# Row maxima of an attention kernel: one transpose of 32 columns in place of four of 8

## The chip, the core and the metric

The kernel runs on one core of a Trainium2 chip. A core has TensorE (PE, matrix products into PSUM; PEld is its loading of the stationary operand), VectorE (DVE), ScalarE (ACT), GpSimd (POOL) and SyncE (SP); transfers between memories are issued from SP, ACT and POOL into queues. Each engine works off its own instructions in order and waits on semaphores for the others. The metric is the device time of one execution in microseconds (us); a lower one is better.

## What is computed

A transformer block on x of shape (2, 1024, 512): layer normalisation, causal attention with 32 heads of 16 and ALiBi biases, and a gate from an octonion feed-forward network with ternary weights. Cut to what matters:

```python
xn = _layernorm(x, axis=-1)
qkv = jnp.einsum('bsd,od->bso', xn, w_qkv) + b_qkv
scores = jnp.einsum('bhqd,bhkd->bhqk', q, k) * scale      # scale = 1/4
scores = scores + alibi[None, :, None, :]                 # per head and key position
scores = jnp.where(causal, scores, -1e9)
attn = jax.nn.softmax(scores, axis=-1)
out = jnp.einsum('bhqk,bkhd->bqhd', attn, v)
s = out @ w_out.T + b_out
g = silu(octonion_ffn(xn))          # gate, up and down with ternary weights
x = x + s * g
```

The case concerns the maximum that the softmax subtracts from each row of scores, and how it gets to where the second score product can use it.

## The kernel before

**Tiling.** Attention is cut into 32 units (b, g, qc): 2 batches, 8 groups of 4 heads, 2 halves of 512 query rows. The scores of a unit are computed twice. The first time (`max_items`, matmul at L537) queries are on the partitions: a tile of 128 queries against up to 512 keys for one head or more. VectorE adds the causal mask on the diagonal block and reduces each row to its maximum. `left` handles the keys of the first half (for qc = 1), `diagonal` the half that has the diagonal. Both write one column for each tile `tl` (4 tiles of 128 queries) and head `i` (4 heads) into small tiles `left` and `mx` of 128 x 16.

The second time (`exp_step`, matmul at L653) keys are on the partitions and queries in the free dimension, so that the result can go straight into the product with the values (`value_step`, L689) after the exponential on ScalarE. The row maximum is subtracted inside this product: the query stack `q_ring` is a tile of 128 rows x 4 heads x 512 queries, whose last two rows (126 and 127, `NR - 2` and `NR - 1`) hold the maxima as a rounded high part and a remainder, against rows of -1 in the key stack. The first product uses rows 0 to 125 only, the second all 128.

**The path of the maxima.** `split_max` joins `mx` and `left` and writes high part and remainder into `rm` on VectorE. `place_max` turns `rm` on TensorE (queries come to lie along the free dimension), copies the result from PSUM to `mr` in SBUF on ScalarE, and issues two transfers on POOL that put the high parts into row 126 of the query stack and the remainders into row 127. The first `exp_step` of the unit waits for both.

**The order.** Instructions of all engines in the attention stage are emitted in one program order that a planner in the kernel computes as it builds the program. It keeps a book of modelled times: `now` for PE, `act`, `dve`, when PSUM buffers come free (`e_free`, `x_free`, `m_free`), and for every unit `placed`, when its maxima lie in the query stack. In each step it takes, among the first products (`next_max`), the second products (`next_exp`), the value products (`next_value`), the turns (`next_turn`: placing maxima, normalising outputs), the projections (`next_side`) and the weight work (`next_behind`), one that is ready soon, by priority. Fills of the query and key stacks on SP (`fill_q`, `fill_k`), the loads of the next projection weights on ACT's queue and the stores of projections follow from the position that the planner has reached. The book entries for `place_max` are in `next_turn`: 436 ns on PE, 150 ns later 500 ns on ACT, and 3500 ns more until the maxima are placed.

**Behind the attention stage** the gated network runs (L1387 gate and up, L1421 down), from about 850 us to the end, without the planner.

Every ACT, DVE, POOL and SP instruction of the first two thirds is issued by a wrapper, so the profile gives all of them one line, L69; they are told apart by their tiles. Matmuls have their own lines. The transposes of `place_max` stand at L602 (`pm` is the PSUM tile, `mr` the copy, `q_stack<-mr` the transfer).

Of the kernel before, what the change touches and what calls it, by code (L numbers as in the profile page):

```python
# [10 lines left out]
F32 = mybir.dt.float32  # L11
F32R = mybir.dt.float32r
BF16 = mybir.dt.bfloat16
AF = mybir.ActivationFunctionType
ALU = mybir.AluOpType
AX = mybir.AxisListType
# [3 lines left out]
P = 128  # L20
# [55 lines left out]
def kernel(  # L76
# [18 lines left out]
    nc = tc.nc  # L95

    held = [True]
    act_, dve_, pool_, sp_ = (
        InOrder(tc, engine, held) for engine in (nc.scalar, nc.vector, nc.gpsimd, nc.sync)
    )  # L100
# [3 lines left out]
    def pe(ins):  # L104

        return tc.keep_in_program_order(ins)
# [14 lines left out]
    wk = ctx.enter_context(tc.tile_pool(name="wk", bufs=2))  # L121
# [5 lines left out]
    ident = const.tile([P, P], F32, name="ident")  # L127
# [86 lines left out]
    for n in range(2):  # L214
        for i in range(4):
            sp_.dma_start(
                out=bqk_sb[n * 64 + i * HD : n * 64 + (i + 1) * HD, :, :],
                in_=bqk[i * 32 : i * 32 + HD, :].rearrange(
                    "d (w g n) -> d w g n", w=2, n=2
                )[:, :, :, n],  # L220
# [177 lines left out]
    def q_of(b, g, half):  # L398
        return q_ring[(2 * (b * NG + g) + half) % 4]

    def k_of(b, g, half):
        return k_ring[(2 * (b * NG + g) + half) % 5]
# [122 lines left out]
    def max_items(b, g, qc):  # L525

        tiles = {}

        def begin():
            for name in ("left", "mx")[1 - qc :]:  # L530
                tiles[name] = wk.tile([P, 4, 4], F32, tag=name, name=f"{name}_{b}_{g}_{qc}")

        def products(tl, first, count, c, n):
            ps = ps_x.tile([P, 512], F32, tag="x", name=f"s1_{b}_{g}_{4 * qc + tl}_{c}_{first}")
            for j in range(count):
                pe(
                    nc.tensor.matmul(  # L537
                        ps[:, j * n : (j + 1) * n],
                        lhsT=q_of(b, g, qc)[0 : NR - 2, first + j, tl * P : (tl + 1) * P],
                        rhs=k_of(b, g, c)[0 : NR - 2, first + j, :n],  # L540
                        start=True,
                        stop=True,
                    )
                )
            return ps[:, 0 : count * n].rearrange("p (h n) -> p h n", n=n)

        def left(tl, i):
            if (tl, i) == (0, 0):
                begin()
            ps = products(tl, i, 1, 0, 512)  # L550
            dve_.tensor_reduce(tiles["left"][:, tl, i : i + 1], ps, AX.X, ALU.max)

        def diagonal(tl, first, count):
            if (qc, tl, first) == (0, 0, 0):
                begin()
            n = (tl + 1) * P
            ps = products(tl, first, count, qc, n)
            block = ps[:, :, tl * P : n]
            dve_.tensor_tensor(
                block,  # L560
                block,
                mask[:, 384:512].rearrange("p (h n) -> p h n", h=1).to_broadcast([P, count, P]),
                ALU.add,
            )
            dve_.tensor_reduce(
                tiles["mx"][:, tl, first : first + count], ps, AX.X, ALU.max
            )

        items = []
        for tl in range(4):  # L570
            if qc:
                for i in range(4):
                    items.append((1, 512, False, lambda tl=tl, i=i: left(tl, i)))
            count = (4, 2, 1, 1)[tl]
            for i in range(0, 4, count):
                items.append(
                    (
                        count,
                        (tl + 1) * P,
                        True,  # L580
                        lambda tl=tl, i=i, count=count: diagonal(tl, i, count),
                    )
                )
        return items, tiles

    def split_max(b, g, qc, tiles):

        mx = tiles["mx"]
        if qc:
            dve_.tensor_tensor(mx, mx, tiles["left"], ALU.max)  # L590
        rm = wk.tile([P, 4, 2, 4], F32, tag="rm", name=f"rm_{b}_{g}_{qc}")
        tiles["rm"] = rm
        dve_.tensor_copy(rm[:, :, 0, :].bitcast(F32R), mx)
        dve_.tensor_tensor(rm[:, :, 1, :], mx, rm[:, :, 0, :], ALU.subtract)

    def place_max(b, g, qc, tiles):

        q = q_of(b, g, qc)
        ps = ps_m.tile([P, 512], F32, tag="m", name=f"pm_{b}_{g}_{qc}")
        for tl in range(4):  # L600
            pe(
                nc.tensor.transpose(  # L602
                    ps[0:8, tl * P : (tl + 1) * P],
                    tiles["rm"][:, tl].rearrange("p l h -> p (l h)"),
                    ident,
                )
            )
        mr = wk.tile([8, 512], F32R, tag="mr", name=f"mr_{b}_{g}_{qc}", bufs=1)
        act_.copy(mr, ps[0:8, :])
        for n in range(2):  # L610
            pool_.dma_start(
                out=q[NR - 2 + n : NR - 1 + n].bitcast(F32),
                in_=mr[4 * n : 4 * n + 4, :].bitcast(F32),
            )

    p_tiles, po_tiles = {}, {}
# [85 lines left out]
    def normalise(b, g, qc):  # L702

        posb = po_tiles.pop((b, g, qc))
        o = op.tile([P, 4, 64], F32, tag="o", name=f"o_{b}_{g}_{qc}")
        pt = ps_m.tile([P, 4, 4, 32], F32, tag="m", name=f"pt_{b}_{g}_{qc}")
        for tl in range(4):
            pe(
                nc.tensor.transpose(
                    pt[:, tl, :, :].rearrange("p h e -> p (h e)"),  # L710
                    posb[:, tl * P : (tl + 1) * P],
                    ident,
                )
            )
        rl = wk.tile([P, 4, 4, 1], F32, tag="rl", name=f"rl_{b}_{g}_{qc}")
        dve_.reciprocal(rl, pt[:, :, :, HD : HD + 1])
        dve_.tensor_tensor(
            o.rearrange("p t (h d) -> p t h d", d=HD),
            pt[:, :, :, 0:HD],
            rl.to_broadcast([P, 4, 4, HD]),  # L720
            ALU.mult,
        )
        n = b * (S // P) + 4 * qc
        sp_.dma_start(
            out=att[n : n + 4, :, g * 64 : (g + 1) * 64].rearrange("t p n -> p t n"), in_=o
        )
# [78 lines left out]
    for u in range(NU):  # L805
        its, t = max_items(*units[u])
# [27 lines left out]
    for b in range(B):  # L834
        for hh in range(2):
            n = 2 * b + hh
# [11 lines left out]
        for gp in range(2 - 2 * b, NP):  # L848
            n = b * NP + gp
# [7 lines left out]
        for n, qc in enumerate((0, 1) if b + 1 < B else (1, 0)):  # L857
            u = (b + 1) * 2 * NG + n

            first, last = (u - 1, u) if b + 1 == B else (u + 8 + 4 * n, u + 12 + 4 * n)  # L860
# [191 lines left out]
    now, kind = [0.0], ["F"]  # L1052
    act, dve = [0.0], [0.0]
    e_free, x_free, m_free = [0.0] * 3, [0.0] * 2, [0.0] * 2
# [6 lines left out]
    def take(pool):  # L1061
        pool.sort()
        return pool

    def run_pe(k, ready, cost):
        now[0] = max(ready, now[0] + SWITCH.get((kind[0], k), 0)) + cost
        kind[0] = k

    def run_act(t, cost):
        act[0] = max(act[0], t) + cost  # L1070
        return act[0]

    def run_dve(t, cost):
        dve[0] = max(dve[0], t) + cost
        return dve[0]
# [79 lines left out]
    def next_turn():  # L1155
        found = []
        if turns:
            u, t = turns[0]

            def go(u=u):  # L1160
                turns.pop(0)
                place_max(*units[u], mtiles[u])
                run_pe("F", ready, 436)
                take(m_free)[0] = run_act(now[0] + 150, 500)
                placed[u] = m_free[0] + 3500

            ready = max(t, min(m_free))
            found.append((ready, 1, 0, go))
        if norms:
            u, t = norms[0]  # L1170

            def go(u=u):
                norms.pop(0)
                normalise(*units[u])
                run_pe("F", t2, 436)
                take(m_free)[0] = run_dve(now[0] + 150, 600)
                stored[units[u]] = m_free[0] + 5000

            t2 = max(t, min(m_free))
            found.append((t2, 2, 0, go))  # L1180
        return [f for f in found if f[0] < HELD]
# [132 lines left out]
    left = [RUN]  # L1314
# [13 lines left out]
    for t in [  # L1328
# [9 lines left out]
        t = t.rearrange("p h n -> p (h n)")[:, 0 : 12 * P]  # L1338
# [122 lines left out]
    for n, (tb, mt) in enumerate(work):  # L1461
# [11 lines left out]
        if n >= 2:  # L1473
            while last_outs:
                _, emit, kind = last_outs.pop(0)
# [76 lines left out]
```

## Time and profile before

| what | us |
|---|---|
| median of 3 runs | 1151.21 (1150.77 to 1151.92) |
| the profiled execution | 1150.65 |
| its span from the first to the last instruction | 1148.9 |
| PE busy | 1067.9 (93%) |
| DVE busy | 679.0 (59%) |
| ACT busy | 500.9 (44%) |
| POOL busy | 176.8 (15%) |
| ACT copies mr<-pm, 32 of 572 ns | 18.3 |
| PE transposes pm<-ident,rm, 128 of 281 ns, overlapping | 20.1 |
| POOL issues q_stack<-mr, 64 of 505 ns | 32.0 |

The mean granted TensorE clock is 0.978. Busy shares are averages over the whole span; PE's is above 0.8 in nearly all 40 slices of the page, that of the others changes with the stage. Durations of matmuls overlap each other, since they are pipelined; what one costs in a row of others is read from the starts in the timeline. `x <- y` in a row is an instruction or transfer that writes tile x and reads y, followed by its shape; `[t <-w]` behind a row is the idle time of the engine before it and what ended it. A chain is followed back from the last instruction, at each step to what released it.

### The profile page before, as it was taken

What the parts mean: (1) busy time and instruction counts of PE and PEld (TensorE: products, weight loads), DVE (VectorE), ACT (ScalarE), POOL (GpSimd) and SP (SyncE); (2) the same over time, 40 slices, a digit from 0 to 9 for tenths busy, and PEclk for the clock granted to TensorE, in tenths of its full rate; (3) what the DMA queues carried; (4) which work ended last, traced back from release to release, by engine and by line L of the source; (5) the groups of instructions that cost most, each with busy time, mean ns of one, the idle gap of its engine ahead of it and who ended that gap; (6) DMA issues with size and microseconds to landing.
All of it is one profiled execution on the core that took longest, in us unless ns stands there. A gap on an engine that the chain in (4) does not pass through costs nothing.

```text
span 1148.9 us, 15597 instructions
## 1 busy us (share of the span) xinstructions
PE 1067.9 (93%) x5562; PEld 680.9 (59%) x5562; DVE 679.0 (59%) x1400; ACT 500.9 (44%) x962; POOL 176.8 (15%) x295
## 2 busy tenths in 40 slices
PE   7979979999999999989999999899889999999996
PEld 5644545664555665545565555555446687878784
DVE  5368787667777687767787768777641123141211
ACT  4122656645554544535435444465582122232222
POOL 6401023100011010010110000001001123242322
PEclk9899979999999999989999999999899999999998
DMA  6975563453744608082542542831041013030200
GB/s 194 206 147 142 112 169 85 69 87 90 140 112 88 127 2 158 2 195 38 140 66 52 102 90 85 142 62 52 25 140 68 29 45 110 1 110 1 76 35 37
DMA packets 73740, 104.24 MB, mean 91 GB/s; under 512 B 26992, under 2 KB 31120, under 8 KB 73664
## 3 DMA queue, kind: packets, MB, share of 16 engines
q1 hardware_dynamic: 66336, 87.48, 34.8%
q10 hardware_dynamic: 3552, 9.78, 2.7%
q0 software_dynamic: 3776, 5.98, 2.1%
q8 instruction: 45, 0.74, 0.3%
q14 instruction: 31, 0.25, 0.1%
HBM read 69.58 MB, written 33.10 MB: 89 GB/s over the span
## 4 chain that ended last, share of the span: by engine, by line
PE 67%; DVE 12%; DMA 9%; ACT 5%; issue 5%; POOL 2%; SPq 1%; ACTq 0%; DVEq 0%; POOLq 0%
PE s L537 11%; PE s L653 11%; PE po L689 11%; PE pqk L466 6%; PE pg L1387 6%; PE pu L1387 6%; PE pd L1421 5%; DVE mx L69 5%; PE pout L758 4%; DMA q_stack<-mr 3%; PE pv L424 3%; DVE s L69 2%; PE s L670 2%; DVE left L69 1%; ACT p L69 1%
## 5 line engine op out<-in xcount | busy, mean ns | idle before, releaser
L69 ACT ACTIVATE p<-s 128x512 f32<-128x512 f32 x576 | 302.3, 599 | 222.7 <-PE s L670 142.0
L537 PE MATMUL s<-k_stack,q_stack 126*128 126x512 f32 (+3 forms) x768 | 276.3, 417 | 28.2 <-DVE mx L69 22.4
L653 PE MATMUL s<-q_stack,k_stack 128*128 128x512 f32 (+3 forms) x768 | 221.5, 373 | 17.3 <-DMA q_stack<-mr 12.9
L69 DVE TENSOR_REDUCE mx<-s 128x1 f32<-128x384 f32 (+3 forms) x352 | 226.2, 643 | 11.7
L69 DVE TENSOR_REDUCE left<-s 128x1 f32<-128x512 f32 x256 | 169.0, 686 | 86.2 <-PE s L537 85.2
L537 PEld LDWEIGHTS s<-k_stack,q_stack 126*128 126x128 f32 x768 | 133.1, 193 | 128.6 <-issue 33.3
L653 PEld LDWEIGHTS s<-q_stack,k_stack 128*128 128x128 f32 x768 | 135.2, 192 | 74.4 <-ACT p L69 30.2
L69 DVE TENSOR_TENSOR s<-s,mask 128x128 f32<-128x128 f32 (+2 forms) x352 | 124.2, 353 | 62.2 <-PE s L537 61.1
L689 PE MATMUL po<-p,v 128*32 128x512 f32 (+3 forms) x1536 | 143.0, 491 | 0.1
L466 PE MATMUL pqk<-xnT,wq 128*128 128x512 f32 x256 | 131.3, 614 | 4.5 <-POOL wq L69 2.2
L69 DVE SCALAR_TENSOR_TENSOR h<-pu,sc_u,sg 128x512 f32<-128x512 f32 (+1 forms) x44 | 33.1, 751 | 166.1 <-PE pu L1387 158.7
L69 POOL DMA_DIRECT2D q_stack<-mr x64 | 32.0, 505 | 583.6 <-ACT mr L69 583.6
L689 PEld LDWEIGHTS po<-p,v 128*32 128x32 f32 x1536 | 43.4, 109 | 78.8 <-issue 67.3
L69 POOL TENSOR_TENSOR hs<-h,hs 128x512 fp32r<-128x512 f32 (+1 forms) x44 | 57.6, 1309 | 190.1 <-ACT hs L69 190.1
L69 ACT ACTIVATE sg<-pg,sc_g 128x512 f32<-128x512 f32 (+1 forms) x44 | 30.2, 687 | 100.2 <-PE pg L1387 95.3
L424 PE MATMUL pv<-wv,xnT 128*128 128x256 f32 x256 | 68.2, 383 | 1.5 <-DVE v L69 1.5
L758 PE MATMUL pout<-wo_sb,oT 128*128 128x512 f32 x128 | 61.1, 597 | 2.0 <-ACT oT L69 1.0
L466 PEld LDWEIGHTS pqk<-xnT,wq 128*128 128x128 f32 x256 | 47.1, 198 | 26.6 <-issue 18.1
L69 ACT CAST hs<-h 128x512 fp32r<-128x512 f32 (+1 forms) x44 | 27.3, 620 | 75.3 <-DVE h L69 75.3
L670 PE MATMUL s<-mask,ident 128*128 128x256 bf16 (+1 forms) x320 | 52.0, 257 | 0.0
L424 PEld LDWEIGHTS pv<-wv,xnT 128*128 128x128 f32 x256 | 45.8, 190 | 9.8 <-issue 3.2
L69 ACT CAST mr<-pm 8x512 fp32r<-8x512 f32 x32 | 18.3, 572 | 70.7 <-PE pm L602 67.2
(142 smaller groups left out, 1081.1 us busy)
## 6 DMA issues: line engine op xcount, KB each, us to landing
sp<-st SPq DMA_DIRECT2D x32, 512.0 KB
k_stack<-sp SPq DMA_DIRECT2D x128, 128.0 KB
q_stack<-sp SPq DMA_DIRECT2D x128, 128.0 KB
wqr<-in_wqk_dram ACTq DMA_DIRECT2D x16, 512.0 KB
xt<-in_x_dram SPq DMA_DIRECT2D x16, 256.0 KB
att<-o SPq DMA_DIRECT2D x32, 128.0 KB
ot<-att SPq DMA_DIRECT2D x16, 256.0 KB
proj<-y SPq DMA_DIRECT2D x16, 256.0 KB
```

The source lines that it names most:

```text
L69: ins = issue(*args, **kwargs)
L424: nc.tensor.matmul(ps[:, 0:256], lhsT=xnT[:, c, b * S + kt * P : b * S + (kt + 1) * P], rhs=wv_tiles[2 * b + hh][:, c, :], start=(c == 0), ...
L466: nc.tensor.matmul(ps, lhsT=wq_tiles[b, gp][:, kt, which, :], rhs=xnT[:, kt, b * S + c * 512 : b * S + (c + 1) * 512], start=(kt == 0), st ...
L537: nc.tensor.matmul(ps[:, j * n : (j + 1) * n], lhsT=q_of(b, g, qc)[0 : NR - 2, first + j, tl * P : (tl + 1) * P], rhs=k_of(b, g, c)[0 : NR ...
L653: nc.tensor.matmul(ps[:, c0 : c0 + w], lhsT=k_of(b, g, kt // 4)[0:NR, h, kt % 4 * P : (kt % 4 + 1) * P], rhs=q[0:NR, h, 512 - w : 512], st ...
L670: pe(nc.tensor.matmul(out, lhsT=ident16, rhs=rhs, start=False, stop=True))
L689: nc.tensor.matmul(po[32 * i : 32 * i + 32, 512 - w : 512], lhsT=v[:, kt, h * VC : h * VC + 32], rhs=p[:, i * part + c0 : i * part + c0 + ...
L758: nc.tensor.matmul(ps, lhsT=turned[t][:, c, :], rhs=wo_sb[0][:, c, :], start=(c == 0), stop=(c == KD - 1),)
L1387: nc.tensor.matmul(ps[:fs, :], lhsT=fw[mt][:, n0 + kt, 0:fs], rhs=part[:, kt, :], start=(kt == 0 and n == 0), stop=(kt == KD - 1 and n == 1),)
L1421: nc.tensor.matmul(pd, lhsT=hs[k][:fs, n, st * P : (st + 1) * P], rhs=fw[mt][:fs, 8:12, :].rearrange("p s n -> p (s n)"), start=(mt == 0 a ...
```

## The change

The 16 columns of maxima are laid out head first, tile last, in place of tile first. `rm` becomes 2 parts x 4 heads x 4 tiles, contiguous: 32 columns that one transpose turns into 32 rows of 128. Before, four transposes turned 8 columns each (2 parts x 4 heads of one tile) into 8 rows x 128 at four places of the free dimension. The copy to SBUF is 32 x 128 in place of 8 x 512. The two transfers each read 16 rows of 128 numbers in place of 4 rows of 512; where they write is the same. The planner's entries for the turn become 109 ns on PE and 200 ns on ACT. No engine's other instructions are edited; their order is what the planner makes of the new entries.

```diff
@@ left, diagonal @@
-            dve_.tensor_reduce(tiles["left"][:, tl, i : i + 1], ps, AX.X, ALU.max)
+            dve_.tensor_reduce(tiles["left"][:, i, tl : tl + 1], ps, AX.X, ALU.max)
...
-                tiles["mx"][:, tl, first : first + count], ps, AX.X, ALU.max
+                tiles["mx"][:, first : first + count, tl], ps, AX.X, ALU.max
@@ split_max @@
-        rm = wk.tile([P, 4, 2, 4], F32, tag="rm", name=f"rm_{b}_{g}_{qc}")
+        rm = wk.tile([P, 2, 4, 4], F32, tag="rm", name=f"rm_{b}_{g}_{qc}")
         tiles["rm"] = rm
-        dve_.tensor_copy(rm[:, :, 0, :].bitcast(F32R), mx)
-        dve_.tensor_tensor(rm[:, :, 1, :], mx, rm[:, :, 0, :], ALU.subtract)
+        dve_.tensor_copy(rm[:, 0].bitcast(F32R), mx)
+        dve_.tensor_tensor(rm[:, 1], mx, rm[:, 0], ALU.subtract)
@@ place_max @@
-        for tl in range(4):
-            pe(
-                nc.tensor.transpose(
-                    ps[0:8, tl * P : (tl + 1) * P],
-                    tiles["rm"][:, tl].rearrange("p l h -> p (l h)"),
-                    ident,
-                )
-            )
-        mr = wk.tile([8, 512], F32R, tag="mr", name=f"mr_{b}_{g}_{qc}", bufs=1)
-        act_.copy(mr, ps[0:8, :])
+
+        pe(nc.tensor.transpose(ps[0:32, 0:P], tiles["rm"].rearrange("p l h t -> p (l h t)"), ident))
+        mr = wk.tile([32, P], F32R, tag="mr", name=f"mr_{b}_{g}_{qc}", bufs=1)
+        act_.copy(mr, ps[0:32, 0:P])
         for n in range(2):
             pool_.dma_start(
                 out=q[NR - 2 + n : NR - 1 + n].bitcast(F32),
-                in_=mr[4 * n : 4 * n + 4, :].bitcast(F32),
+                in_=mr[16 * n : 16 * n + 16, :].bitcast(F32),
             )
@@ next_turn @@
                 place_max(*units[u], mtiles[u])
-                run_pe("F", ready, 436)
-                take(m_free)[0] = run_act(now[0] + 150, 500)
+                run_pe("F", ready, 109)
+                take(m_free)[0] = run_act(now[0] + 150, 200)
                 placed[u] = m_free[0] + 3500
```

## The prediction

> **What bounds the kernel now.** I read the page's chain of waits first, to see which engine sets the end, then the group rows of the turned tile, then the chain piece by piece in stretches of 100 us, last the timeline around single placements.
>
> ```profile
> PE 67%; DVE 12%; DMA 9%; ACT 5%; issue 5%; POOL 2%; SPq 1%; ACTq 0%; DVEq 0%; POOLq 0%
> PE s L537 11%; PE s L653 11%; PE po L689 11%; PE pqk L466 6%; PE pg L1387 6%; PE pu L1387 6%; PE pd L1421 5%; DVE mx L69 5%; PE pout L758 4%; DMA q_stack<-mr 3%; PE pv L424 3%; DVE s L69 2%; PE s L670 2%; DVE left L69 1%; ACT p L69 1%
> ```
>
> TensorE holds two thirds of the chain, and one transfer, the placement of the row maxima (q_stack<-mr), stands in it with 3%. The attention stage runs from about 50 to 850 us. The table of windows over it gives 747 us of busy PE in 800, so 53 us of idle at most. A matmul instruction taken away there should mostly shorten the kernel; what shortens only ACT or POOL should not.
>
> ```profile
> L602 PE MATMUL pm<-ident,rm x128: 269/272/421, 69.9 to 826.5; 128*8 128x128 f32 x128
> L69 ACT CAST mr<-pm x32: 558/575/579, 70.7 to 826.9; 8x512 fp32r<-8x512 f32 x32
> ```
>
> This view of the turned tile (min, median and max ns; first and last start in us) shows 128 transposes and 32 copies. A transpose lasts 272 ns, but they overlap, so the timeline must say what four cost:
>
> ```profile
> 498.16 0.60 PE L602 MATMUL pm<-ident,rm 128*8 128x128 f32 x4
> ...
> 498.59 1.02 PE L466 MATMUL pqk<-xnT,wq 128*128 128x512 f32 x2
> ...
> 499.66 0.98 POOL L69 DMA_DIRECT2D q_stack<-mr  x2 [6.36 <-ACT mr L69]
> ...
> 507.11 1.19 PE L653 MATMUL s<-q_stack,k_stack 128*128 128x512 f32 x2 [3.56 <-DMA q_stack<-mr]
> ```
>
> Four transposes hold PE from 498.16 until the next matmul starts at 498.59, 0.43 us. The copy starts when the last has ended, POOL issues two transfers, and at 507.11 PE has stood still for 3.56 us until they landed.
>
> ```profile
> 498.24 0.53 PE pm L602 x4
> ...
> 498.79 0.58 ACT mr L69
> ...
> 500.15 6.83 DMA q_stack<-mr
> ```
>
> These are the chain's pieces at the same placement (start, length): transposes, copy and transfer are all on it. The same view, asked for the whole stage in stretches, has the transposes on the chain at 24 of the 32 units (1 unit is one placement), the copy at 10 and the transfer at 7.
>
> **The change part by part.** *TensorE.* Three of four transposes of each unit go, 96 in all. At the eight placements for which I asked the timeline, four take 0.35 to 0.44 us to the next matmul's start, so one takes 0.09 to 0.11 and three fewer give 0.26 to 0.33; I take 0.30. The one that stays loads 32 columns in place of 8: nearest rows 86 ns for 8 and 110 ns for the 32 columns of the value products (po); 24 ns more, under the running matmul. 24 units on the chain x 0.30 = 7.2 us. The other 8, where the chain runs through VectorE, give 0 to 0.33 each; I take 0, since another engine ends last.
>
> *ScalarE.* The copy goes from 8x512 to 32x128. Its nearest row is the 80x128 cast out of PSUM of the down weights (md), 263 ns: 572 - 263 = 0.31 us less, 32 times. ACT has idle time enough, so only the chain counts. At three of its ten places there (160.15, 173.77 and 826.85) the next link is again work of PE or ACT: 3 x 0.31 = 0.9 us.
>
> *The seven placements that PE waits for.* Transposes and copy together bring the issue 0.30 + 0.31 = 0.61 us forward.
>
> ```profile
> q_stack<-mr POOLq DMA_DIRECT2D x64, 8.0 KB, 1.8
> ...
> mw<-md POOLq DMA_DIRECT2D x4, 40.0 KB, 1.9
> ```
>
> The usual landing is 1.8 us, but the seven on the chain take 3.69 to 6.83 us: they share the DMA engines with bulk traffic (the DMA share is 1.1 in 500 to 510 us). If the landing follows the issue, each gives 0.61; if it comes when the bulk has drained, 0, and the 0.30 counted above for the six of them with transposes on the chain is lost again. I take the middle: 7 x 0.31 / 2 = 1.1 us gained, 6 x 0.30 / 2 = 0.9 us taken back.
>
> *The transfers.* Two per unit as before, on POOL, from 16 rows of 512 B in place of 4 rows of 2 KB. The second row above, of 80 rows of 512 B bounds it: it lands 0.1 us later, and its issue takes 0.56 us beside 0.50. So 0 to 0.1 us in landing and 0 to 0.12 in the two issues, at seven places 0 to 1.5 us; 16 rows are nearer to 4 than to 80, I take 0.2. Queued behind them on POOL are only weight repacking and memsets, with 583.6 us of idle in front of these transfers. Queue 0 shows 64 packets for the two transfers of one placement (549 to 555 us), 32 each. A rule speaks against the change here: the Trainium skill, "DMA: Bandwidth & Descriptors", section "Why a DMA increments its semaphore by 16 and not by 1", spreads data over as many engines, up to 16, as divide the slowest dimension on both sides, which could make 4 rows use 4 engines and 16 rows up to 16, to wait for the most backlogged of them. The same section lets all 16 engines report the end of a transfer issued from GpSimd whatever its shape, and 32 packets for 4 rows look like that; by the first alone the seven landings could lose what they gain, by the second nothing, and the sum stays.
>
> *VectorE.* The reductions write their columns with a stride, the split writes contiguously. The cast into the strided rm takes 175 ns, the contiguous maximum of mx and left 175 ns: nothing.
>
> *The planner.* Its book entries for one placement fall by 327 ns on PE and 300 on ACT, so every later greedy choice may fall differently, in all queues, SP's fills included. The trace of before cannot show the new order. Bounds from the waits:
>
> ```profile
> PE s L537 <- DVE mx L69: 22.4, 55, 3.3
> ...
> PE s L653 <- DMA q_stack<-mr: 12.9, 7, 3.6
> ```
>
> If the seven waits vanished, 12.9 us would go; if there were twice as many, 12.9 would come. I take 0 and keep both for the rivals.
>
> **Sum:** 7.2 + 0.9 + 1.1 - 0.9 - 0.2 = 8.1 us. The profiled execution took 1150.65 us (span 1148.9 and 1.75 around it); 1142.55 after. The median of the runs is 0.56 above it: 1143.1. Without the order, the ends are 18 x 0.26 - 1.5 = 3.2 us and 24 x 0.33 + 10 x 0.31 + 8 x 0.33 = 13.7 us: 1137.5 to 1148.
>
> **The rivals.** *A, slower: the new order makes PE wait for more placements.* The place is the first score product with the maxima row (L653) of a unit. The books land a placement 3.5 us after the copy; the timeline has 499.36 to 506.98 us, 7.6. A wait costs 12.9 / 7 = 1.84 us. 8.1 / 1.84 = 4.4, so five more waits turn the gain into a loss and six put it past 2.3 us. With eight more: 1151.2 - 8.1 + 14.7 = 1157.8. For it: the order is a chain of greedy choices, and seven of 32 are late today. Against: transposes, copy and books shrink together, so the books become no worse than they are.
>
> *B, hidden anyway.* VectorE sets the pace: maxima over 512 columns take 691 ns on DVE against 473 ns for the matmul, and DVE is busy 593 of 800 us of the stage. If PE's freed slots all become waits for mx, only the copies' 0.9 us are left: 1150.3. Against it: the chain has DVE at 12% and PE at 67%.
>
> *C, a larger gain: the clock.*
>
> ```profile
> 505.00:510.00 5.00, 2.89 (x6) 2.05 (x7) 0.86 (x2) 2.03 (x4) 0.00 (x0) 0.53 1.10 191
> 510.00:515.00 5.00, 5.00 (x15) 2.94 (x13) 2.95 (x7) 3.41 (x8) 0.00 (x0) 0.79 0.45 170
> 555.00:560.00 5.00, 3.60 (x15) 2.65 (x15) 3.10 (x8) 3.03 (x7) 0.00 (x0) 1.00 0.88 169
> ```
>
> The column after the five engines is the granted clock. After the 3.56 us gap it is 0.53, then 0.79; after the 1.59 us gap at 556 it stays 1.00. The other gap of this kind (3.52 us, ending at 78.6) has 0.86 and 0.80 over 75 to 85 us. Together 5 x (0.47 + 0.21 + 0.14 + 0.20) = 5.1 us of clock, part of it while PE stood. If both gaps fall below the point between 1.59 and 3.52 where the clock gives way, and all landings follow their issues (3 us more than taken), 1143.1 - 5.1 - 3 = 1135. The Trainium skill's "TensorE: Matmul & The Clock Gate", section "HAM oscillation — how this bites in real kernels", sets that point near 3.4 us; by it 0.6 us less would be enough and the sum would be up to 5.1 lower. The rows leave it open, so the forecast has nothing for it.
>
> **How the numbers follow.** The forecast of 1143.1 has a chance of 0.50 (own range 1137.5 to 1148), A 0.25, B 0.15, C 0.10. About 0.2% (2.3 us) is what a measurement can tell from no change. Faster: 0.50 + 0.10 and 0.02 of B, 0.62; slower: nearly all of A, 0.24; the rest, 0.14, within. The range 1135 to 1157 cuts half of A above and half of C below, under 2 in 10.
>
> **What would show it.** Right: L602 with 32 transposes on 32 columns and 0.09 to 0.11 us to the next matmul; a copy near 0.26 us; median landing 1.8 to 1.9; the attention stage some 8 us shorter, the part behind it as long as before. Wrong: more than seven waits of L653 for q_stack<-mr, or more than 12.9 us in them (A); waits for DVE mx and left up by as much as L602 lost (B). A landing above 2.3 us, or a copy no shorter than 0.5, would break the steps themselves.

## The result and the profile after

The changed kernel takes 1164.57 us (median of 4 runs, 1160.96 to 1171.03) against 1151.57: a ratio of 1.012, 95% interval 1.0088 to 1.0153. It is slower by 13 us where 8 less were forecast. The profiled execution took 1160.96 us, its span is 1159.2, so the readings below explain a loss of 10.3 us against the profile of before. The runs of this kernel differ by 10 us among themselves, those of before by 2.

First the chain of waits on the page of the changed kernel, by engine and by line:

```profile
PE 65%; DVE 13%; issue 7%; DMA 6%; ACT 5%; POOL 2%; SPq 0%; ACTq 0%; POOLq 0%; DVEq 0%
PE s L537 11%; PE po L683 11%; PE s L647 10%; PE pqk L466 7%; PE pg L1381 6%; PE pu L1381 6%; PE pd L1415 5%; DVE mx L69 5%; PE pout L752 4%; PE pv L424 3%; DVE s L69 2%; DVE left L69 2%; PE s L664 2%; ACT p L69 2%; DMA q_stack<-mr 1%
```

(Behind the edit, lines are up to six lower: L653 is now L647, L689 is L683.) The placement fell from 3% to 1% of the chain; PE's share fell by two points. So the time did not go into the path that was edited. The turned tile, in the columns used before:

```profile
L601 PEld LDWEIGHTS pm<-ident,rm x32: 94/95/103, 69.9 to 838.0; 128*32 128x32 f32 x32
L601 PE MATMUL pm<-ident,rm x32: 269/273/372, 70.0 to 838.2; 128*32 128x128 f32 x32
L69 ACT CAST mr<-pm x32: 237/254/256, 70.8 to 839.1; 32x128 fp32r<-32x128 f32 x32
```

32 transposes instead of 128, the copy at 254 ns where it was 575, the weight load at 95 ns where it was 86. The timeline of PE around one placement of the changed kernel gives the price of the transpose that is left, from its start to the next start:

```profile
458.09 0.27 PE L601 MATMUL pm<-ident,rm 128*32 128x128 f32 x1
458.20 1.02 PE L466 MATMUL pqk<-xnT,wq 128*128 128x512 f32 x2
```

0.11 us here; 0.03 us at 69.99 and at 488.09, where a score product follows. And the transfers of the changed kernel land as before (KB each, median us from issue to landing):

```profile
q_stack<-mr POOLq DMA_DIRECT2D x64, 8.0 KB, 1.7
```

So the transposes of a unit, the copy and the landing all became cheaper. The waits of PE in the attention stage (50 to 860 us; total, times, longest) show where the time went:

```profile
PE s L537 <- DVE mx L69: 17.0, 43, 1.1
PE s L647 <- ACT p L69: 15.8, 6, 13.4
PE pqk L466 <- POOL wq L69: 5.8, 4, 3.5
PE s L647 <- DMA q_stack<-mr: 4.6, 3, 3.0
PE s L537 <- DVE left L69: 4.5, 4, 3.7
```

The same view of before has 12.9 us in 7 for the placements, 1.4 in 4 for left, and:

```profile
PE s L653 <- ACT p L69: 3.4, 6, 1.3
PE pqk L466 <- POOL wq L69: 2.2, 2, 1.9
```

The wait for placements fell from 12.9 us in 7 to 4.6 us in 3. Two single waits are new: one of 13.4 us for an exponential and one of 3.5 us for compacted projection weights. (The 3.7 us for `left`, at 152.5 us, stands where before PE waited 3.3 us for `mx`, at 154.1 us.) Everything before 284 us runs level with before: the copies of the maxima start within 3 us of the old ones, at 284 us 0.4 us earlier. At the next unit they are 8.3 us late, at 466 us 22.6, at 827 us 12.2. Behind the attention stage nothing changed: from the first gate product to the end it is 277.5 us in both.

### The long stall

The pieces of the chain between 463 and 481 us in the changed kernel (start, length), those of ACT and SP that only issue mostly left out:

```profile
463.49 1.21 ACT p L69 x3
...
465.19 4.43 DMA wqr<-in_wqk_dram
...
469.68 0.30 SPq L69
...
472.52 6.24 DMA sp<-st
...
478.86 0.69 ACT st L69
479.55 0.49 ACT p L69
...
480.09 1.28 PE s L647 x2
```

This is read from the bottom. PE waits for an exponential that frees a PSUM bank. The exponential stands in ACT's queue behind `st`, the evacuation of a projection. `st` waits until one of the two staging buffers has been stored (sp<-st). That store is late in SP's queue, and SP was held up by a transfer on ACT's queue: `wqr`, the load of the next pair's query and key weights. SP's own timeline in the same kernel:

```profile
443.75 0.23 SPq L69 DMA_DIRECT2D k_stack<-al_dram  x1
468.44 0.38 SPq L69 DMA_DIRECT2D att<-o  x1
469.68 1.71 SPq L69 DMA_DIRECT2D q_stack<-sp  x4
...
472.52 0.46 SPq L69 DMA_DIRECT2D sp<-st  x1
```

SP issues nothing from 443.98 to 468.44 us. The view of its waits (total, times, longest) puts 24.4 us of this down to wqr:

```profile
SPq L69 <- DMA wqr<-in_wqk_dram: 46.0, 6, 24.4
```

The attention outputs that it stores next (att<-o) were ready from 440.4 us on, and they have nothing to do with projection weights. The compiled program tells the link (what four of its transfers wait for, names shortened; DMAHW0 to 7 are semaphores that count landed transfers):

```
SP   att<-o_6_1          [waits DMAHW4, DVE]
SP   q_stack<-sp         [waits DMAHW5, PE]
ACT  wqr_2 first half    [waits DMAHW1, DMAHW4, DMAHW0, Pool]
ACT  wqr_2 second half   [waits DMAHW5]
```

Transfers of SP and ACT take eight semaphores in turn, and each waits for the earlier user of its own. The halves of this load have numbers 4 and 5; six SP transfers later the numbers come round, and att<-o and q_stack<-sp wait for the two halves. The packets of the halves end at 468.0 and 469.3 us in the trace, and the two transfers were issued at 468.44 and 469.68 us, 0.4 us behind each. The load itself stands in ACT's queue behind exponentials that wait for PE, and was issued only from 464.81 us on, 21 us after SP had reached its own next transfer.

The other new wait is the same load one pair earlier (timeline of the changed kernel):

```profile
306.38 0.82 ACTq L69 DMA_DIRECT2D wqr<-in_wqk_dram  x2
...
310.04 1.00 POOL L69 COPY wq<-wqr 128x128 f32<-128x128 f32 x4 [24.82 <-DMA wqr<-in_wqk_dram]
...
311.62 1.22 PE L466 MATMUL pqk<-xnT,wq 128*128 128x512 f32 x1 [3.48 <-POOL wq L69]
```

Here the weights are simply needed 5 us after the load was issued, and PE stands for 3.48 us. After both stalls the granted clock is low: 0.59 and 0.73 over 310 to 320 us, 0.50 over 480 to 485. In full-speed time that is 5 x (0.41 + 0.27) = 3.4 and 5 x 0.5 = 2.5 us, part of it while PE stood. 13.4 + 3.5 + 3.4 + 2.5 = 22.8 us; less the forecast saving of 8.1, a loss of 14.7 is left, where the profiled runs show 10.3 and the medians 13. That the two are near is no proof: the sum leaves out the waits that became shorter (8.3 us for placements, 2.3 for mx and left) and the clock that was low before.

The windows give the whole balance. Up to the first gate product, the stage from 50 us on lasts 831.7 us where it was 821.4. PE is idle in it for 66.0 us where it was 55.2, and busy for 765.7 where it was 766.2, though 96 transposes are gone; the granted clock is 0.96 where it was 0.98. So the loss stands in the profile as longer idle time, and the saving on PE went to the lower clock.

So the reading is: the edit saves what it should, and the planner's new entries draw a new program order in which the weight load comes late twice. A rival has to be excluded: that the 32-column form costs something on the chip itself.

### The profile page after: what moved, and what is told of

The parts are those of the page before. It is cut to its first block, busy times and chain, and to the rows that moved or that the text cites. A ratio compares the mean times of both kernels' runs of the same rounds, so it can differ in the third digit from the quotient of the medians.

```text
span 1159.2 us, 15408 instructions
## 1 busy us (share of the span) xinstructions
PE 1067.4 (92%) x5466; PEld 675.2 (58%) x5466; DVE 678.0 (58%) x1400; ACT 490.9 (42%) x962; POOL 175.6 (15%) x295
## 3 DMA queue, kind: packets, MB, share of 16 engines
q1 hardware_dynamic: 66336, 87.48, 34.5%
## 4 chain that ended last, share of the span: by engine, by line
PE 65%; DVE 13%; issue 7%; DMA 6%; ACT 5%; POOL 2%; SPq 0%; ACTq 0%; POOLq 0%; DVEq 0%
PE s L537 11%; PE po L683 11%; PE s L647 10%; PE pqk L466 7%; PE pg L1381 6%; PE pu L1381 6%; PE pd L1415 5%; DVE mx L69 5%; PE pout L752 4%; PE pv L424 3%; DVE s L69 2%; DVE left L69 2%; PE s L664 2%; ACT p L69 2%; DMA q_stack<-mr 1%
## 5 line engine op out<-in xcount | busy, mean ns | idle before, releaser
L537 PE MATMUL s<-k_stack,q_stack 126*128 126x512 f32 (+3 forms) x768 | 283.5, 427 | 25.9 <-DVE mx L69 17.0
L647 PE MATMUL s<-q_stack,k_stack 128*128 128x512 f32 (+3 forms) x768 | 220.5, 371 | 21.4 <-ACT p L69 15.8
L647 PEld LDWEIGHTS s<-q_stack,k_stack 128*128 128x128 f32 x768 | 136.8, 193 | 68.2 <-ACT p L69 38.8
L683 PE MATMUL po<-p,v 128*32 128x512 f32 (+3 forms) x1536 | 144.5, 498 | 0.6 <-ACT p L69 0.5
L683 PEld LDWEIGHTS po<-p,v 128*32 128x32 f32 x1536 | 43.3, 110 | 78.1 <-issue 69.1
L69 ACT ACTIVATE st<-pqk,bqk_sb 128x512 fp32r<-128x512 f32 x32 | 22.0, 689 | 101.3 <-PE pqk L466 83.9
L69 DVE SCALAR_TENSOR_TENSOR st<-pqk,bqk_sb,st 128x512 fp32r<-128x512 f32 x32 | 24.0, 750 | 54.7 <-ACT st L69 54.7
```

Of the source, the lines that this page charges most:

```text
L69: ins = issue(*args, **kwargs)
L537: nc.tensor.matmul(ps[:, j * n : (j + 1) * n], lhsT=q_of(b, g, qc)[0 : NR - 2, first + j, tl * P : (tl + 1) * P], rhs=k_of(b, g, c)[0 : NR ...
L647: nc.tensor.matmul(ps[:, c0 : c0 + w], lhsT=k_of(b, g, kt // 4)[0:NR, h, kt % 4 * P : (kt % 4 + 1) * P], rhs=q[0:NR, h, 512 - w : 512], st ...
L683: nc.tensor.matmul(po[32 * i : 32 * i + 32, 512 - w : 512], lhsT=v[:, kt, h * VC : h * VC + 32], rhs=p[:, i * part + c0 : i * part + c0 + ...
```

## Experiments

Each ratio is to the kernel before, run beside it on the same chip.

### Form and order apart

**e1_old_books**: the changed kernel with the old entries. Apart from the turns themselves, TensorE's order is then instruction for instruction that of before.

```diff
-                run_pe("F", ready, 109)
-                take(m_free)[0] = run_act(now[0] + 150, 200)
+                run_pe("F", ready, 436)
+                take(m_free)[0] = run_act(now[0] + 150, 500)
```

> The changed transposes, copy and transfers with the planner's old entries (436 and 500 ns), so the program order is that of before. Theory 1 (the loss comes from the new order alone, and the local steps save what was forecast): 1143 us, 1138 to 1147, a ratio near 0.993. Theory 2 (the 32-column form itself costs time on the chip, through its transfers or its wait): at or above 1158 us, a ratio of 1.006 or more.

**e2_new_books**: the kernel before with the new entries, the same two lines edited the other way round.

> The old four transposes, copy and transfers with the planner's new entries (109 and 200 ns), so the order is that of the changed kernel. Theory 1: the losses of the new order without the savings, 1164.6 + 8 = about 1172 us, 1163 to 1180, with a stall of TensorE above 8 us between 450 and 500 us. Theory 2: about 1151 us, as before.

| us, median (ratio, interval) | old order | new order |
|---|---|---|
| four transposes | 1151.87 | 1170.37 (1.0161, 1.0145 to 1.0177) |
| one transpose | 1144.55 (0.993, 0.9906 to 0.9953) | 1164.57 (1.012, 1.0088 to 1.0153) |

Both came out as theory 1 had it. The form saves 7.3 us in the old order and 5.8 in the new; the order costs 18.5 and 20.0. The stall follows the order, not the form: without any edited operation e2_new_books has it too, in its timeline at the same place.

```profile
469.89 0.44 ACTq L69 DMA_DIRECT2D wqr<-in_wqk_dram  x1
...
484.51 0.69 ACT L69 ACTIVATE st<-pqk,bqk_sb 128x512 fp32r<-128x512 f32 x1 [14.25 <-DMA sp<-st]
...
485.74 1.28 PE L653 MATMUL s<-q_stack,k_stack 128*128 128x512 f32 x2 [14.37 <-ACT p L69]
```

The same sequence of load, `st` behind a store, and a second score product that has waited 14.37 us. Theory 2 is out.

### The weight load

**e3_wq_pool**: the changed kernel; TensorE's order is untouched, the load goes to another queue.

```diff
-                load_wq((n // NP, n % NP), act_)
+                load_wq((n // NP, n % NP), pool_)
```

> The changed kernel with the loads of the next projection weights (wqr) issued on POOL's queue in place of ACT's; TensorE's order is untouched. Theory 1a (nearly all of the loss are the two stalls behind a late wqr load, 3.48 us at 308 and 13.43 us at 467, and the low clock after them): both go, 1164.6 - 17 - 4 = about 1143 us, 1139 to 1149. Theory 1b (the new order loses a little everywhere): 1158 us or more, the stall at 467 gone or not.

Measured: 1142.37 us (0.9924, 0.9904 to 0.9943), 22.2 us less than the changed kernel. The windows over the place of the stall (busy us of PE, PEld, DVE, ACT, POOL, granted clock, DMA share, GB/s), first in the changed kernel:

```profile
465.00:470.00 5.00, 1.66 (x7) 0.85 (x5) 0.00 (x0) 0.55 (x2) 0.00 (x0) 1.00 0.69 236
470.00:475.00 5.00, 0.00 (x0) 0.00 (x0) 0.00 (x0) 0.00 (x0) 0.00 (x0) 0.63 0.90 130
475.00:480.00 5.00, 0.00 (x0) 0.00 (x0) 0.42 (x1) 1.14 (x3) 0.00 (x0) 0.50 0.96 272
480.00:485.00 5.00, 4.91 (x19) 1.30 (x19) 2.13 (x5) 2.01 (x5) 0.00 (x0) 0.50 0.67 255
```

and in e3_wq_pool:

```profile
465.00:470.00 5.00, 4.76 (x28) 2.20 (x30) 4.34 (x9) 4.51 (x10) 1.54 (x5) 1.00 0.24 56
470.00:475.00 5.00, 4.58 (x34) 3.04 (x27) 3.34 (x6) 1.78 (x4) 1.38 (x6) 1.00 0.46 62
475.00:480.00 5.00, 5.00 (x46) 3.08 (x45) 3.64 (x7) 2.10 (x5) 0.00 (x0) 1.00 0.02 5
480.00:485.00 5.00, 5.00 (x31) 3.20 (x31) 3.73 (x9) 3.55 (x7) 0.00 (x0) 1.00 1.06 148
```

In the changed kernel TensorE, VectorE and POOL do nothing for five us and more, while transfers are busy; the clock halves. With the load moved the same stretch is full, and in the whole execution SP has no wait for wqr left.

**e4_wq_early**: the load stays on ACT's queue, but is issued behind the first of a pair's four groups of projection products, where it stood behind the third (first pair) or fourth.

```diff
-            if (which, c, kt) == (1, n > 1, KD - 1) and n < B * NP:
+            if (which, c, kt) == (0, 0, KD - 1) and n < B * NP:
```

> The changed kernel with the wqr loads still on ACT's queue, but emitted behind the first projection product of the pair before and not behind its sixth or eighth of sixteen groups or the last; TensorE's order is untouched. If lateness of the load in ACT's queue is what counts: as with the loads on POOL's queue, about 1143 us, 1139 to 1149. If sharing of the semaphores of ACT's and SP's transfers is what counts, however early the load: a stall of SP for wqr remains and the time stays above 1155 us. Theory 1b: 1158 us or more.

Measured: 1149.55 us (0.9975, 0.9956 to 0.9994), just above the 1139 to 1149 that was expected. The stall at 467 us is gone, though SP still has 64.7 us of waits for wqr in 12: the shared semaphores alone do not stop PE. It is 7 us behind e3_wq_pool. Against the kernel before, its placements are 3 us late by 71 us and 10.5 by 329, where e3_wq_pool is 0.6 and 2.9 late. So the early load costs something in the first third; I did not trace it further.

**e13_wq_sp**: the changed kernel with the load on SP's queue.

```diff
-                load_wq((n // NP, n % NP), act_)
+                load_wq((n // NP, n % NP), sp_)
```

> The changed kernel with the wqr loads on SP's queue: they still share semaphores with SP's other transfers, but no longer stand behind the exponentials on ACT's queue. If the place on ACT's queue makes the load late: the stall at 467 us is gone, 1140 to 1149 us. If the shared semaphores are the cause whatever the queue: a stall of TensorE above 8 us stays, above 1155 us.

Measured: 1147.60 us (0.9961, 0.9946 to 0.9976), no stall at 467 us. It has one wait of 5.9 us of its own, at 96 us, for compacted weights. But its load is hardly earlier than in the changed kernel:

```profile
458.34 0.36 SPq L69 DMA_DIRECT2D sp<-st  x1
...
463.69 1.30 SPq L69 DMA_DIRECT2D wqr<-in_wqk_dram  x2
...
468.00 0.69 ACT L69 ACTIVATE st<-pqk,bqk_sb 128x512 fp32r<-128x512 f32 x1
```

It was issued from 463.69 us on, where the changed kernel has 464.81 (e3_wq_pool 454.29, e4_wq_early 431.80); its work runs 2.5 us behind the changed kernel's at the last placement before. What differs is the place: in SP's own queue the load stands behind att<-o and behind the store that `st` waits for, so neither can wait for it, and `st` ran without a wait. So two things are shown. Bringing the load forward removes the stall (e3_wq_pool, e4_wq_early), and so does leaving it nearly as late with SP's transfers ahead of it (e13_wq_sp). The long stall does not come from the lateness by itself, but through the SP transfers that wait for the load. That they wait through the semaphore numbers is read from the program and the landing times; no run changes the numbers alone, or the two staging buffers.

### Is it the size of the entries?

**e5_pe_entry** and **e6_act_entry**: the changed kernel with only one entry lowered.

```diff
e5:              run_pe("F", ready, 109)
e5:              take(m_free)[0] = run_act(now[0] + 150, 500)
e6:              run_pe("F", ready, 436)
e6:              take(m_free)[0] = run_act(now[0] + 150, 200)
```

> The one transpose of 32 columns, the planner's entry for PE at 109 ns, that for ACT left at 500. TensorE's order differs both from before and from the changed kernel. Theory 3 (any change of an entry draws a new order, and a stall falls in it or not by chance): somewhere from 1140 to 1165 us, with stalls at other places than 308 and 467 us. Theory 4 (the smaller entry for PE is what makes the weight load late): as the changed kernel, 1158 us or more, with a stall of TensorE above 8 us.

> The one transpose of 32 columns, the planner's entry for PE left at 436 ns, that for ACT at 200. Theory 3: somewhere from 1140 to 1165 us, stalls at other places than 308 and 467 us. Theory 4: the stall above 8 us is gone, 1141 to 1148 us.

Measured: 1147.60 us (0.997, 0.9955 to 0.9984) and 1156.94 us (1.0042, 1.0026 to 1.0059). Neither has the long stall; the largest waits of PE in the later part are 2.71 us at 492 in the one, 3.37 at 500 and 3.15 at 518 in the other. Theory 4 falls: the lower PE entry alone does not bring the long stall. Theory 3 held, but its range of 25 us left little that could have broken it. With the same form four orders take 1144.55, 1147.60, 1156.94 and 1164.57 us.

**e12_entry_430**: the kernel before with one number changed.

```diff
-                run_pe("F", ready, 436)
+                run_pe("F", ready, 430)
```

> The kernel before with one number changed in the planner, the entry for PE from 436 to 430 ns; no operation differs, the order does. If the order alone moves the time: outside 1149.5 to 1154 us, to either side, up to 15 us. If a new order is neutral as a rule and the changed kernel had bad luck only in its size: 1151.8, within 2.3 us.

Measured: 1152.97 us (1.0012, 0.9999 to 1.0025), not told apart from before, though 1291 of the program's 4451 matmuls and transposes stand at another place in TensorE's order. So this miss counts against the strong form of theory 3: a new order need not move the time.

### Does the load matter in the old order, and do the gains add up?

**e7_before_wq_pool**: the kernel before with the load on POOL's queue. **e8_old_books_wq_pool**: e1_old_books with the same edit, that of e3_wq_pool.

> The kernel before with the wqr loads on POOL's queue. If the late load hurts only in the new order: 1151, as before, 1148 to 1153 us. If the waits of SP for wqr that the kernel before has too (84.5 us in 8) reach TensorE there: 1141 to 1147 us, with fewer waits of TensorE for q_stack and wq.

> The one transpose of 32 columns, the old entries (so the order of before) and the wqr loads on POOL's queue. If form and queue add up: the time of the same kernel with the load on ACT's queue, 1144.5 us, less what the load's move gives the kernel before; 1144 if that is nothing, 1138 if it is 6 us.

Measured: 1144.46 us (0.9941, 0.9919 to 0.9963) and 1136.94 us (0.9873, 0.9838 to 0.9907). The move gives 7.3 us beside the kernel before (1151.75 in these runs) and 7.6 beside e1_old_books, the form 7.5 with the load moved: they add up. The old order had its own late load, at 500 us, where the forecast had read a wait for a placement. Windows there, first of e1_old_books, then of e8_old_books_wq_pool:

```profile
500.00:510.00 10.00, 6.42 (x18) 3.53 (x17) 5.63 (x13) 2.76 (x5) 0.77 (x2) 0.87 0.99 213
```

```profile
500.00:510.00 10.00, 9.63 (x39) 4.80 (x41) 8.48 (x20) 6.93 (x13) 0.00 (x0) 1.00 0.29 109
```

PE is busy for 9.63 of 10 us where it was 6.42, and the DMA engines for 0.29 of the time where it was 0.99: the load and the fills that had piled up behind it no longer coincide with the placement. Between the placements that stood at 499 and 518 us before, e8_old_books_wq_pool gains 5.6 us on the kernel before. The length of SP's hold is no measure of the loss: this load holds SP for 34.5 us before, longer than the 24.4 of the changed kernel, and the longest wait of PE is 3.56 us. What counts is which transfers stand behind it. e8_old_books_wq_pool beats both kernels, by 1.3% (interval 0.9838 to 0.9907) and, from the medians, 2.4%.

**e10_pe_entry_pool**, **e11_act_entry_pool**: e5 and e6 with the load on POOL's queue.

> The one transpose of 32 columns, entries 109 and 500, wqr loads on POOL's queue. Theory 5 (what tells the orders apart is where the late load falls; without it they are nearly alike): between the two orders already seen with the load on POOL's queue, 1136 to 1143 us. Theory 6 (orders differ as much by themselves): 1147.6 less the 7 us that the move gave the kernel before, and the difference between this and the next run stays near 9 us.

> The one transpose of 32 columns, entries 436 and 200, wqr loads on POOL's queue. Theory 5: 1136 to 1143 us, some 15 us below the same order with the load on ACT's queue. Theory 6: 1156.9 - 7 = about 1150 us.

Measured: 1138.29 us (0.988, 0.9865 to 0.9894) and 1146.15 us (0.9957, 0.994 to 0.9973). Theory 5 holds for the first and fails for the second, which lies between the two theories; the difference between the two orders is 7.9 us, nearly the 9 that theory 6 had. All four orders with the load on either queue:

| entries PE, ACT | load on ACT's queue | on POOL's queue | gain |
|---|---|---|---|
| 436, 500 (old) | 1144.55 | 1136.94 | 7.6 |
| 109, 500 | 1147.60 | 1138.29 | 9.3 |
| 436, 200 | 1156.94 | 1146.15 | 10.8 |
| 109, 200 (new) | 1164.57 | 1142.37 | 22.2 |

The spread of the orders falls from 20 to 9 us. Of the 20.0 us that the new order costs with one transpose, 14.6 go with the load's move and 5.4 stay (1142.37 against 1136.94). What is left of the spread does not come from the load's place on ACT's queue, and its source is open: the order of 436, 200 is already 13 and 11 us late at 264 us, with the load on the one queue and on the other. In both columns an ACT entry of 200 is slower than one of 500 beside the same PE entry, by 4.1 to 17.0 us. Whether a lower ACT entry does this as a rule, or four orders fell so by chance, no run here decides.

## Why the prediction was wrong, step by step

- **Three transposes fewer, 0.30 us a unit.** Four took 0.35 to 0.44 us to the next matmul's start at the places read, one takes 0.03 to 0.11: about 0.33 less. Right, a little small.
- **The copy, 0.31 us less.** 575 to 254 ns: right; its nearest row, 263 ns, was the right one.
- **The transfers, 0 to 0.1 us later.** 1.8 to 1.7 us, and an issue of 488 ns where it was 505. Right that nothing is lost; the 0.2 us was no cost at all. That 16 rows might have to wait for more engines than 4 shows in no median; the landings that came late are another matter.
- **The seven placements that PE waits for.** In the old order (e1_old_books) 11.4 us in 6 waits are left of 12.9 in 7. The middle between "follows the issue" and "drains with the bulk" was fair. What I did not see is what the bulk was: e7_before_wq_pool shows that at 500 us it hung on the late weight load.
- **VectorE: nothing.** rm takes 175 ns as before.
- **The sum of 8.1 us.** With the order held it is 7.3, with the load moved 7.5. The sum of the costed steps was right. Part of what rival B had feared came with it: in e1_old_books the waits for mx and left are 27.7 us, 3.9 more than before. So the total does not confirm each term.
- **The planner.** This is the step that failed: "I take 0 and keep both for the rivals", with bounds of 12.9 us to either side. The order costs 18.5 us with the old form and 20.0 with the new. The bounds were made from the waits that the edited path already had, and so could only hold more or fewer of those. The loss came through a queue that the edit does not touch: one load on ACT's queue, late behind exponentials, held SP for 24.4 us and so PE for 13.4, and 14.6 of the 20.0 us go when it is moved. The other 5.4 are not traced. I had named "all queues, SP's fills included" and then costed none of them. Yet the view of SP's waits before shows the coupling of SP to ACT's queue, though not what it would cost in another order:

```profile
SPq L69 <- DMA wqr<-in_wqk_dram: 84.5, 8, 34.5
```

- **Rival A** had the sign and the cause, a recomputed order, but not the mechanism: the waits for placements became fewer, and one wait cost 13.4 us, not the mean of 1.84.
- **Rival B**: waits for mx and left are 21.5 us where they were 23.8. Not it.
- **Rival C**: the gap before 78 us shrank from 3.52 to 3.03, and the clock over 75 to 85 us stayed low, 0.88 and 0.78. No gain came from there.

## What to carry to other kernels

When an edit also changes the inputs of a scheduler, split it before judging it: the new operations in the old order and the old operations in the new order are two runs, and they tell a saving of 7 us from an order that costs 20. Do not bound the effect of a new order by the waits on the edited path alone; look at every queue that waits for another, above all for a large transfer issued from a compute engine's queue, where it stands behind work that waits. Here moving such a load to another queue was worth as much as the change itself in the old order, 7.3 us, and 22.2 us in the new one; over the four orders it halved the spread.

## What was not expected

The forecast had looked for a length of gap, between 1.59 and 3.52 us, from which the granted clock falls. There is no single one: it fell around a gap of 2.19 us (0.94, then 0.72; e4_wq_early at 330 us) and one of 2.71 (0.97, then 0.69; e5_pe_entry at 492), but not around one of 2.91 (1.00; e1_old_books at 362). A section of the Trainium skill, "HAM oscillation — how this bites in real kernels" in "TensorE: Matmul & The Clock Gate", speaks of idle gaps above some 3.4 us; here the longest gap alone does not say whether the clock falls.

A transpose of 32 columns in front of a score product holds TensorE for 0.03 us, less than the 0.09 us that each of four in a row took.
